# Layer 0 of a scan-and-memory kernel: m's norm by rows in eight blocks, and group statistics in steps a unit apart

## The chip, the cores and the metric

The kernel runs on one core of a Trainium2 chip. Its time is the device time of one execution in microseconds (us); three timed runs gave 5054.97, 5055.22 and 5063.75, median 5055.22. [...]SP issues nearly all DMAs. The engines are called PE (TensorE), DVE (VectorE), ACT (ScalarE), POOL (GpSimd) and SP in the profile.

## The reference, cut to what matters

Two layers act on x of shape (2, 512, 64, 64), that is 2 batches, 512 channels and 4096 positions.

```python
x = x + mamba(gn(x))          # layer 0: a selective scan over the 4096 positions
x = x + memory(gn(x), m)      # layer 1: soft lookup in m (1024 rows of 512)

def gn(v):                    # 32 groups of 16 channels
    g = v.reshape(B, 32, 16, H, W)
    return ((g - mean(g)) / sqrt(var(g) + 1e-5)).reshape(v.shape)   # mean, var over a group and all positions

def memory(x, m):
    xn, mn = l2norm(tokens(x)), l2norm(m)      # l2norm divides each row by its length
    score = xn @ mn.T
    new_m = 0.999 * m + 0.001 * mean of the tokens whose best row it is
    return softmax(score) @ new_m
```

Two small pieces of this are what the change touches: mn, the rows of m divided by their length, which layer 1 needs as a matrix with channels on the partitions; and the mean and the inverse root of the variance of the 32 groups, once for each batch and each layer. All else stays.

## The kernel before, in words

Layer 0 is cut into 32 chunks of 256 positions (16 for each batch). A chunk is cut into 32 units: 8 blocks of 128 inner channels times 4 groups of 4 states. The number of a unit within its chunk is what "unit 12" means below. For each unit the main loop (from line 939) does the same things: `decay` writes exp(delta A) into PSUM on ACT (tile dA), one unit ahead; `feed` makes the scan's input on POOL (tile bu), four units ahead, with four buffers; `scan` runs the recurrence on DVE; `weigh` multiplies by C on DVE (tile hc, two buffers), or on POOL for units 2, 8, 12, 16 and 26; `gather` adds hc up on PE by transposes into tile yT. So hc can be written again only when PE has gathered what stood there two before, and a late PE stops DVE.

Everything else is placed between the units by a table of (unit, priority, function), built from line 911 on. `AT` (line 179) gives the units: the projections u and z of the next chunk (tile pz), the convolution (cv), the small projection (px), the layer norm of the chunk after that, the softplus of delta in eight steps (`d_mm` to `d_first`, with a series in tile q on POOL), and the output projection of the chunk before (po). The class `Queue` (line 26) stamps every instruction of layer 0 so that each engine keeps exactly the order in which they are written; this is why they all show line 36 in the profile, and tile names are used to tell them apart. Each engine thus works down one fixed queue, and an instruction that waits holds up all behind it.

Nearly all of these extra products share two PSUM buffers (tag "mm" of pool `ps`, line 203): a third tile waits until one of the two has been read for the last time.

`unit_m` (line 650) runs in four chunks, 8 to 11, for 256 rows of m each. It loads the transposed m (`mT`, channels on partitions), squares it on ACT, sums the squares over the channels by four matmuls with a constant matrix (tile pn), has the root on DVE and ACT, refines it by one Newton step on POOL (tile rm, 128x256), multiplies m by it on POOL (128x1024), and stores it to the DRAM tensor mnd. Its places are units 2, 28, 28, 30, 31 and 32, so that the last one falls into the next chunk.

`group_stats` (line 152) runs four times: for layer 0 at the start (batch 0) and at unit 12 of chunk 0 (batch 1), both through `stats_end` (line 215), which also makes gsh, the shift; and for layer 1 in `end` (line 630), at unit 23 of chunk 16 for batch 0 and behind the last chunk for batch 1. It joins the statistics of each channel on DVE (tiles gs_mv and gs_w), averages over the 16 channels of a group by a matmul (gs_pm), forms the spread on DVE (gs_d), averages that by a second matmul (gs_pv), takes the root on ACT and refines it on DVE (`rsqrt`, line 143). All of it is issued in one go, so that DVE's queue holds the steps back to back.

`clear` writes zeros over the two tables of layer 1 at unit 12 of chunk 1; it shares a tile with m.

Of the kernel before, what the change touches and what calls it, by code (L numbers as in the profile page):

```python
# [8 lines left out]
F32 = mybir.dt.float32  # L9
# [3 lines left out]
AF = mybir.ActivationFunctionType  # L13
# [5 lines left out]
P = 128  # L19
EPS = 1e-5  # L20
# [29 lines left out]
def kernel(  # L50
# [15 lines left out]
    mT: bass.AP,  # L66
# [76 lines left out]
    def rsqrt(nc, dst, var, work):  # L143

        nc.scalar.activation(dst, var, AF.Ln, bias=epsc)
        nc.scalar.activation(dst, dst, AF.Exp, scale=-0.5)
        nc.vector.tensor_mul(work, dst, dst)
        nc.vector.scalar_tensor_tensor(work, var, EPS, work, ALU.add, ALU.mult)
        nc.vector.tensor_scalar(work, work, -0.5, 1.5, ALU.mult, ALU.add)
        nc.vector.tensor_mul(dst, dst, work)  # L150

    def group_stats(nc, st, mu, rs, pool, psum):

        mv = pool.tile([P, CB, 2], F32, tag="gs_mv", name="gs_mv")
        for cb in range(CB):
            nc.vector.bn_aggr(mv[:, cb, :], st[:, cb].rearrange("p n s -> p (n s)"))
        w = pool.tile([P, CB, 2], F32, tag="gs_w", name="gs_w")
        pm = psum.tile([P, 2, T], F32, tag="mm", name="gs_pm")
        nc.vector.tensor_copy(w[:, :, 0], mv[:, :, 0])
        nc.tensor.matmul(pm[:, 0, :CB], gmat, w[:, :, 0], start=True, stop=True)  # L160
        nc.vector.tensor_copy(mu, pm[:, 0, :CB])
        d = pool.tile([P, CB], F32, tag="gs_d", name="gs_d")
        nc.vector.tensor_sub(d, mv[:, :, 0], mu)
        nc.vector.tensor_mul(d, d, d)
        nc.vector.tensor_add(d, d, mv[:, :, 1])
        pv = psum.tile([P, 2, T], F32, tag="mm", name="gs_pv")
        nc.tensor.matmul(pv[:, 0, :CB], gmat, d, start=True, stop=True)
        d2 = pool.tile([P, CB], F32, tag="gs_d2", name="gs_d2")
        rsqrt(nc, rs, pv[:, 0, :CB], d2)
# [4 lines left out]
    with ExitStack() as l0:  # L174
# [14 lines left out]
            "wo": (5, 1, 8, 7), "m": (2, 28, 28, 30, 31, 32), "gs": 12, "zo1": (-4, -3, -1, 3),  # L189
# [25 lines left out]
        def stats_end(b):  # L215
            group_stats(nc, st0, gmu[0][b], grs[0][b], s1, ps)
            nc.vector.tensor_mul(gsh[b], gmu[0][b], grs[0][b])
            nc.vector.tensor_scalar_mul(gsh[b], gsh[b], -1.0)
# [83 lines left out]
        stats_end(0)  # L302
# [288 lines left out]
        def back_fns(i):  # L591
# [38 lines left out]
            def end():  # L630
                if c == NCH - 1:
                    group_stats(nc, sts[b], gmu[1][b], grs[1][b], s1, ps)
                state[i].clear()
# [3 lines left out]
        def back(i):  # L637
# [10 lines left out]
            return parts + [(AT["end"], end)]  # L648

        def unit_m(q):  # L650

            s = {}
            cols = slice(q * T, (q + 1) * T)

            def load_m():
                s["m"] = s1.tile([P, CB, T], F32, tag="m", name="m")
                nc.sync.dma_start(
                    s["m"], mT[:, cols].rearrange("(cb p) k -> p cb k", p=P)
                )

            def square(h):
                sq = s1.tile([P, 2, T], F32, tag="sq", name="sqm")
                nc.scalar.activation(sq, s["m"][:, 2 * h : 2 * h + 2], AF.Square)
                if h == 0:
                    s["pn"] = ps.tile([P, 2, T], F32, tag="mm", name="pn")
                for j in range(2):
                    cb = 2 * h + j
                    nc.tensor.matmul(
                        s["pn"][:, 0], meanc, sq[:, j], start=cb == 0, stop=cb == CB - 1
                    )  # L670
# [557 lines left out]
```

## Time and profile before

| what | value |
|---|---|
| timed runs, median | 5055.22 us (5054.97 to 5063.75) |
| profiled execution, own time | 5066.93 us |
| its span | 5065.2 us, mean granted PE clock 0.966 |
| busy shares PE, PE weight load, DVE, ACT, POOL | 89, 69, 80, 70, 75% |
| layer 0, main loop | 130.2 to 3977.4 us |
| layer 1 | from about 3985 us to the end |
| chunk 0, chunk 1 | 149.8 and 117.4 us |

A line of a group in the profile gives the source line, the engine and operation, the output and input tiles, shapes and number, then busy time, mean duration, and idle time of that engine just before, with what ended the idle time. A line of the timeline gives start, duration, engine, operation, and in brackets the idle time before it and what ended that. A line of the table by stretches gives the stretch, its length, the busy time of PE, PE weight load, DVE, ACT and POOL with the number of instructions, the mean granted PE clock (1.00 is full speed), the share of the DMA engines that was busy and GB/s.

### The profile page before, as it was taken

The page shows a single profiled execution, that of the slowest core. Times are in us where ns is not written, and L with a number is a line of the kernel's source. Part 1 is how long each engine was busy: PE and PEld are TensorE (multiplying, and loading weights), DVE is VectorE, ACT ScalarE, POOL GpSimd, SP SyncE. Part 2 cuts the span into 40 slices and gives each one's busy share as a digit, 9 for nine tenths or more (in the row PEclk, how much of TensorE's full clock was granted, in tenths as well). Part 3 has the DMA queues.
Part 4 walks back from the last instruction along what each step waited for, and adds up shares of the span by engine and source line. Part 5 has one row for each costly group of instructions (what it writes and reads, how often), then busy time and mean ns, then how long its engine had stood idle before and what let it go on. Part 6 is the DMA issues. An engine that isn't in the chain of part 4 may idle for free. (4 is left out here: it accounts for less than half of the span.)

```text
span 5065.2 us, 64865 instructions
## 1 busy us (share of the span) xinstructions
PE 4523.6 (89%) x22704; PEld 3500.2 (69%) x22704; DVE 4048.3 (80%) x3390; ACT 3533.2 (70%) x8845; POOL 3822.4 (75%) x2825
## 2 busy tenths in 40 slices
PE   6888888988888899989898888888986899998999
PEld 5677777777777777777777777777775555553444
DVE  3699999999988999999999999999998755553010
ACT  1688888888888888878888888888886555551000
POOL 3799999999999999989999999999999322220000
PEclk9899999999999999999999999999997899998999
DMA  5022221122222212121122221221112344334453
GB/s 198 19 100 77 80 80 63 63 72 73 74 71 69 65 64 65 63 63 63 63 72 84 75 73 63 67 70 64 64 61 98 117 158 149 131 134 142 144 163 119
DMA packets 174400, 447.73 MB, mean 88 GB/s; under 512 B 23256, under 2 KB 77656, under 8 KB 169848
## 3 DMA queue, kind: packets, MB, share of 16 engines
q1 hardware_dynamic: 160384, 408.50, 24.0%
q0 software_dynamic: 10240, 34.61, 2.2%
q8 instruction: 179, 2.93, 0.2%
q14 instruction: 149, 1.22, 0.1%
q10 hardware_dynamic: 3448, 0.47, 0.1%
HBM read 351.63 MB, written 91.88 MB: 88 GB/s over the span
## 5 line engine op out<-in xcount | busy, mean ns | idle before, releaser
L36 POOL TENSOR_TENSOR bu<-B,du 128x1020 f32<-128x1020 f32 (+1 forms) x1152 | 2453.2, 2146 | 127.8 <-DVE dA L36 102.1
L36 ACT ACTIVATE dA<-delta,A 128x256 f32<-128x256 f32 x4096 | 1957.9, 478 | 150.5 <-DVE hc L36 39.8
L36 DVE TENSOR_TENSOR_SCAN dA<-dA,bu 128x1024 f32<-128x1024 f32 x864 | 1977.9, 2289 | 35.9 <-ACT dA L36 16.7
L36 PE MATMUL yT<-ident,hc 128*128 128x128 f32 x8192 | 1063.5, 278 | 193.0 <-DVE hc L36 109.8
L36 DVE TENSOR_TENSOR hc<-dA,C 128x1024 f32<-128x1024 f32 x864 | 1058.5, 1225 | 164.5 <-PE yT L36 76.0
L36 PEld LDWEIGHTS yT<-ident,hc 128*128 128x128 f32 x8192 | 950.2, 143 | 281.2 <-DVE hc L36 137.2
L36 PE MATMUL pz<-x,win 128*128 128x256 f32 x4096 | 938.5, 382 | 42.6 <-ACT bu L36 23.8
L36 PEld LDWEIGHTS pz<-x,win 128*128 128x128 f32 x4096 | 763.2, 191 | 153.4 <-POOL bu L36 27.8
L36 PE MATMUL po<-z,wo 128*128 128x256 f32 x2048 | 523.5, 414 | 1.8 <-DMA wo<-in_out_wT_dram 1.1
L36 PE MATMUL cv<-xi,cd 128*128 128x256 f32 x2048 | 473.6, 384 | 29.2 <-POOL xi L36 22.9
L36 PEld LDWEIGHTS po<-z,wo 128*128 128x128 f32 x2048 | 424.2, 210 | 83.3 <-issue 15.3
L1163 PE MATMUL po<-exT,win 128*128 128x512 f32 x1024 | 444.4, 597 | 20.3 <-DVE win L1146 14.3
L36 PEld LDWEIGHTS cv<-xi,cd 128*128 128x128 f32 x2048 | 382.1, 191 | 91.5 <-POOL xi L36 28.9
L1096 PE MATMUL pc<-win,xf 128*128 128x512 f32 x960 | 432.3, 592 | 0.0
L36 DVE TENSOR_TENSOR_SCAN h<-dA,bu 128x1024 f32<-128x1024 f32 x160 | 364.9, 2280 | 21.8 <-ACT dA L36 19.9
L1163 PEld LDWEIGHTS po<-exT,win 128*128 128x128 f32 x1024 | 196.1, 192 | 268.0 <-issue 268.0
L36 POOL TENSOR_TENSOR hc<-h,C 128x1024 f32<-128x1024 f32 x160 | 379.4, 2372 | 0.5 <-PE yT L36 0.5
L1070 POOL DMA_INDIRECT tab<-rows,ix x64 | 62.8, 982 | 418.2 <-DVE den L1111 398.6
L36 ACT COPY carry<-dA 128x4 f32<-128x4 f32 x810 | 130.1, 161 | 348.9 <-DVE hc L36 343.2
L1180 DVE TENSOR_TENSOR xt<-xt,po 128x512 f32<-128x512 f32 x64 | 44.0, 687 | 389.0 <-PE po L1163 373.2
L1096 PEld LDWEIGHTS pc<-win,xf 128*128 128x128 f32 x960 | 173.0, 190 | 172.2 <-issue 172.2
L36 PE MATMUL py<-ident,ys 128*128 128x128 f32 x512 | 85.8, 292 | 188.7 <-DVE q L36 70.0
(161 smaller groups left out, 5070.2 us busy)
## 6 DMA issues: line engine op xcount, KB each, us to landing
B<-bcd SPq DMA_DIRECT2D x128, 512.0 KB, 4.3
C<-bcd SPq DMA_DIRECT2D x128, 512.0 KB, 4.3
wo<-in_out_wT_dram SPq DMA_DIRECT2D x128, 512.0 KB, 5.0
exd<-exT SPq DMA_DIRECT2D x16, 2048.0 KB, 6.3
exT<-exd SPq DMA_DIRECT2D x16, 2048.0 KB, 9.2
xl<-in_x_dram SPq DMA_DIRECT2D x32, 512.0 KB, 6.3
x<-in_x_dram SPq DMA_DIRECT2D x32, 512.0 KB, 5.3
xo<-in_x_dram SPq DMA_DIRECT2D x64, 256.0 KB, 5.7
```

The source lines that it names most:

```text
L36: ins = call(*args, **kwargs)
L1070: nc.gpsimd.indirect_dma_start(tab, at, rows, None)
L1096: nc.tensor.matmul(pc[:, cols], xf[:, cb, i * P : (i + 1) * P], mn[:, cb, cols], start=cb == 0, stop=cb == CB - 1,)
L1163: nc.tensor.matmul(pos[j, cb], mrow[:, kb, cb * P : (cb + 1) * P], ld[j][0][:, kb], start=kb == 0, stop=kb == KB - 1,)
L1180: nc.vector.tensor_add(xt[:, cb], xt[:, cb], pos.pop((j, cb)))
```

## The change

m's norm is done by rows. Eight blocks of 128 rows are handled in chunks 8 to 15, one in each. A block is loaded as it lies (rows on partitions, 256 KB), squared on ACT with the sum of each row as by-product, so that the root and its Newton step work on one number for each partition (128x1, POOL and ACT). ACT then scales the rows, PE turns the block by four 128x128 transposes into an "mm" PSUM tile (ptm), ACT copies it out and SP stores it to mnd. The places are units 3, 12, 13, 14, 22 and 23. The input mT is gone.

`group_stats` returns a list of four steps: means, variances, roots, newton. The second and the fourth use the engine that is passed in: POOL for batch 1 of layer 0 and batch 0 of layer 1, DVE for the two that have nothing beside them. The variance is first copied from PSUM to SBUF by ACT. In chunk 0 the steps stand at units 12, 12, 13, 14, and the shift at 15; in chunk 16 at units 23, 24, 25, 26. From the second step on (in chunk 0 from the first on) they carry priority -1, so they come ahead of all else at their unit. `clear` uses a smaller tile (528 instead of 1024 columns).

```diff
+    def group_stats(nc, engine, st, mu, rs, pool, psum):
+        s = {}
+        def means():
+            mv = s["mv"] = pool.tile([P, CB, 2], F32, tag="gs_mv", name="gs_mv")
+            for cb in range(CB):
+                nc.vector.bn_aggr(mv[:, cb, :], st[:, cb].rearrange("p n s -> p (n s)"))
+            w = pool.tile([P, CB, 2], F32, tag="gs_w", name="gs_w")
+            nc.vector.tensor_copy(w[:, :, 0], mv[:, :, 0])
+            s["pm"] = psum.tile([P, 2, T], F32, tag="mm", name="gs_pm")
+            nc.tensor.matmul(s["pm"][:, 0, :CB], gmat, w[:, :, 0], start=True, stop=True)
+        def variances():
+            mv = s["mv"]
+            nc.vector.tensor_copy(mu, s.pop("pm")[:, 0, :CB])
+            d = s["d"] = pool.tile([P, CB], F32, tag="gs_d", name="gs_d")
+            engine.tensor_sub(d, mv[:, :, 0], mu)
+            engine.tensor_mul(d, d, d)
+            engine.tensor_add(d, d, mv[:, :, 1])
+            s["pv"] = psum.tile([P, 2, T], F32, tag="mm", name="gs_pv")
+            nc.tensor.matmul(s["pv"][:, 0, :CB], gmat, d, start=True, stop=True)
+        def roots():
+            nc.scalar.copy(s["d"], s.pop("pv")[:, 0, :CB])
+            s["v"] = s["d"]
+            nc.scalar.activation(rs, s["v"], AF.Ln, bias=epsc)
+            nc.scalar.activation(rs, rs, AF.Exp, scale=-0.5)
+        def newton():
+            work = pool.tile([P, CB], F32, tag="gs_d2", name="gs_d2")
+            v = s.pop("v")
+            engine.tensor_mul(work, rs, rs)
+            engine.tensor_scalar(v, v, 1.0, EPS, ALU.mult, ALU.add)
+            engine.tensor_mul(work, v, work)
+            engine.tensor_scalar(work, work, -0.5, 1.5, ALU.mult, ALU.add)
+            engine.tensor_mul(rs, rs, work)
+        return [means, variances, roots, newton]
...
-            "wo": (5, 1, 8, 7), "m": (2, 28, 28, 30, 31, 32), "gs": 12, "zo1": (-4, -3, -1, 3),
+            "wo": (5, 1, 8, 7), "m": (3, 12, 13, 14, 22, 23), "gs": 12, "zo1": (-4, -3, -1, 3),
...
+        def unit_m(kb):
+            rows = slice(kb * P, (kb + 1) * P)
             def load_m():
+                s["m"] = s1.tile([P, C], F32, tag="m", name="m")
+                nc.sync.dma_start(s["m"], m[rows])
+            def square():
+                s["ss"] = s1.tile([P, 2], F32, tag="mss", name="mss")
+                junk = s1.tile([P, ROW], F32, tag="mj", name="mj")
+                nc.scalar.activation(junk[:, :C], s["m"], AF.Square, accum_out=s["ss"][:, 0:1])
             def root():
+                ss, r = s["ss"][:, 0:1], s["ss"][:, 1:2]
+                nc.gpsimd.tensor_scalar(ss, ss, 1e-24, None, ALU.max)
                 nc.scalar.activation(r, ss, AF.Ln)
                 nc.scalar.activation(r, r, AF.Exp, scale=-0.5)
             def newton():
+                ss, r = s["ss"][:, 0:1], s["ss"][:, 1:2]
                 nc.gpsimd.tensor_mul(ss, ss, r)
                 nc.gpsimd.tensor_mul(ss, ss, r)
                 nc.gpsimd.tensor_scalar(ss, ss, -0.5, 1.5, ALU.mult, ALU.add)
                 nc.gpsimd.tensor_mul(r, r, ss)
+            def turn():
+                nc.scalar.mul(s["m"], s["m"], s["ss"][:, 1:2])
+                pt = s["pt"] = ps.tile([P, 2, T], F32, tag="mm", name="ptm")
+                pt = pt.rearrange("p a t -> p (a t)")
+                for cb in range(CB):
+                    nc.tensor.transpose(
+                        pt[:, cb * P : (cb + 1) * P], s["m"][:, cb * P : (cb + 1) * P], ident
+                    )
+            def store():
+                mt = s.pop("m")
+                nc.scalar.copy(mt, s.pop("pt").rearrange("p a t -> p (a t)"))
+                nc.sync.dma_start(mnd[:, :, rows], mt.rearrange("p (c k) -> p c k", k=P))
...
-        M_AT = [len(chunks) // 4 + q for q in range(K // T)]
+        M_AT = [len(chunks) // 4 + kb for kb in range(KB)]
...
+                parts = back(i - 1)
+                table += [(at + n, 4, fn) for n, fn in parts[:-3]]
+                table += [(at + n, -1, fn) for n, fn in parts[-3:]]
...
-        table.append((AT["gs"], 5, lambda: stats_end(1)))
+        table += [(AT["gs"] + max(n - 1, 0), -1, fn) for n, fn in enumerate(stats_end(1))]
```

## The prediction

> **What bounds the kernel now.** I read the page's 40 slices first. From slice 3 to slice 30 (layer 0) VectorE, GpSimd and TensorE all stand at 8 to 9 tenths and ScalarE at 8; TensorE alone sets the pace only after 3990 us. Slices are too coarse for this change, so I cut layer 0 at the first scan of each chunk (its start is in VectorE's timeline) and asked for busy times chunk by chunk. Below are chunks 6 to 13 and 16; the columns are the stretch, its length, then PE, PEld, DVE, ACT, POOL busy, granted clock, DMA.
>
> ```profile
> 867.80:986.20 118.40, 106.53 (x610) 91.73 (x609) 112.39 (x76) 100.46 (x260) 113.14 (x83) 0.97 0.21 68
> 986.20:1102.60 116.40, 103.40 (x610) 89.52 (x609) 112.29 (x75) 100.49 (x260) 113.05 (x83) 1.00 0.21 69
> 1102.60:1222.10 119.50, 107.72 (x623) 93.07 (x622) 112.94 (x77) 102.02 (x264) 115.69 (x86) 0.99 0.22 72
> 1222.10:1348.70 126.60, 112.37 (x618) 96.42 (x617) 113.10 (x76) 102.18 (x264) 117.95 (x88) 0.93 0.22 72
> 1348.70:1474.40 125.70, 111.43 (x617) 95.49 (x616) 113.07 (x75) 102.16 (x264) 117.84 (x88) 0.95 0.22 72
> 1474.40:1601.20 126.80, 112.54 (x618) 96.57 (x617) 113.14 (x76) 102.27 (x264) 118.00 (x88) 0.93 0.21 72
> 1601.20:1724.20 123.00, 108.57 (x604) 93.14 (x603) 112.47 (x74) 100.62 (x260) 115.38 (x85) 0.94 0.22 69
> 1724.20:1840.90 116.70, 104.82 (x610) 90.57 (x609) 112.36 (x75) 100.50 (x260) 113.11 (x83) 0.99 0.21 69
> ...
> 2075.30:2201.20 125.90, 109.50 (x623) 94.81 (x622) 115.87 (x88) 99.96 (x253) 113.39 (x78) 0.95 0.20 64
> ```
>
> The length column is the point. A plain chunk takes 116 to 118.4 us; the 14 chunks from 2201.2 to 3846.6 average 1645.4 / 14 = 117.5. In a plain chunk VectorE (112.4) and GpSimd (113.1) both have about 4 us to spare, ScalarE 17. Chunks 8 to 12, which hold m's old norm, take 621.6, that is 34.1 more than 5 x 117.5. Chunk 16, with the group statistics of batch 0, takes 8.4 more.
>
> Why 34? GpSimd gained only 3 x 0.73 + 0.41 + 2.36 = 5.0 us a unit (the rows of rm and m), 20 in all. TensorE's timeline early in chunk 10 shows the rest; the columns are start, duration, instruction, idle before it.
>
> ```profile
> 1362.75 1.09 PE L36 MATMUL yT<-ident,hc 128*128 128x128 f32 x8
> 1367.21 1.09 PE L36 MATMUL yT<-ident,hc 128*128 128x128 f32 x8 [3.37 <-POOL hc L36]
> ...
> 1372.43 5.20 PE L36 MATMUL cv<-xi,cd 128*128 128x256 f32 x16
> ```
>
> GpSimd, 5 us late, gives hc late; TensorE idles 3.37 us; its granted clock then reads 0.71 and 0.50 in the next two stretches of 3.4 us, so 16 matmuls take 5.20 instead of 3.62, and VectorE, which needs yT done before it may write hc again, stalls at units 6 and 7. So a delay of GpSimd is multiplied by the clock.
>
> For the statistics, VectorE in chunk 16:
>
> ```profile
> 2160.27 1.92 DVE L36 BATCH_NORM_AGGREGATE gs_mv<-st 128x2 f32<-128x96 f32 x4
> 2162.22 0.17 DVE L36 COPY gs_w<-gs_mv 128x4 f32<-128x4 f32 x1
> 2166.03 0.16 DVE L36 COPY gmu<-gs_pm 128x4 f32<-128x4 f32 x1 [3.63 <-PE gs_pm L36]
> ...
> 2168.81 2.29 DVE L36 TENSOR_TENSOR_SCAN dA<-dA,bu 128x1024 f32<-128x1024 f32 x1
> ```
>
> From 2160.35 to 2168.81 no scan runs: 2.1 us of aggregates, 3.6 waiting for the matmul behind the u projection, and 2.8 for the two roundtrips after it.
>
> **The change, part by part.**
>
> *m, removed.* All of the 34.1 us: both 0.42 us tensor_scalars and 5.0 us of GpSimd a unit, and the clock loss they cause.
>
> *m, added, per block, eight blocks in chunks 8 to 15.* ScalarE: Square 0.63 plus its accumulator read 0.19 (the rows of junk, lines 1030), Ln 0.26 and Exp 0.21 (the grs rows, 128x4), the scaling 0.59 and the copy from PSUM 0.59 (the row of xT, 128x512): 2.5 us. TensorE: four transposes, 0.14 apart as in the yT rows (8 in 1.09): 0.6. GpSimd: five operations on 128x1. No row has that shape; the ends are the 128x2 memset (0.10) and the 128x32 tensor_tensor (0.25), each plus the 0.08 that dependent GpSimd operations leave between them, so 0.9 to 1.65; I take the 128x6 copy (0.19), the nearest size: 1.35. SP: one 256 KB load at unit 3 and one 256 KB store at unit 23, half of what they were and twice as many; the load waits for nothing new, the store waits for the copy at 23, and behind it on SP stands nothing due before unit 24. Zero; without that cover the landing is some 5 us and still nobody needs m before unit 12.
>
> ScalarE has 17 us a chunk free, so its 2.5 are not a bound by themselves. What counts is who waits at the two places.
>
> *Units 12 to 17.* Behind the five small operations on GpSimd stand two feeds and the softplus series q. In chunk 15 (no stall before it):
>
> ```profile
> 2017.68 1.28 POOL L36 TENSOR_TENSOR q<-q,e 128x512 f32<-128x512 f32 x1
> ...
> 2019.30 0.67 DVE L36 SCALAR_TENSOR_TENSOR q<-lg,q 128x512 f32<-128x512 f32 x1
> ```
>
> q ends at 2018.96, VectorE asks at 2019.30: 0.34 to spare. With 1.35 more VectorE waits 1.0, and the hc of unit 18 some 0.2 more. ScalarE's square and roots (1.3) push the dA of unit 17 from 0.9 early to about 0.5 late: inside the same wait. But in every second chunk VectorE has already lost 2.38 us at unit 14 to the halved clock, and there q is 2.8 early: cost 0. In chunks like 13 (0.7 lost) it is about 0.3. With half the chunks of the first kind: 0.5 x 0 + 0.25 x 0.3 + 0.25 x 1.2 = 0.4.
>
> *Units 22 to 25.* The transposes need one of the two "mm" PSUM buffers. At unit 22 one holds z's last projection until unit 26, the other u's first until xi is copied at unit 23. So TensorE's transposes, issued at 22, wait for that copy, with the yT gathers of units 22 and 23 behind them; and ScalarE's store copy at 23 waits for the transposes, with the decay of unit 25 behind it. ScalarE in chunk 13:
>
> ```profile
> 1813.93 0.59 ACT L36 COPY xi<-pz 128x512 f32<-128x512 f32 x1 [1.17 <-PE pz L36]
> ...
> 1814.61 2.01 ACT L36 ACTIVATE dA<-delta,A 128x256 f32<-128x256 f32 x4
> 1816.56 0.58 ACT L36 COPY ys<-yT 128x512 f32<-128x512 f32 x1
> ```
>
> The scaling (0.59) fits into the 1.17 idle. Then: xi ends 1814.52, transposes done 1815.3 (0.07 + 0.7), copied 1816.0, the two small copies 1816.2, dA done 1818.2 instead of 1816.62. VectorE's scan of unit 25 starts at 1816.90 in the trace; it would start at 1818.3: 1.4 us a chunk. GpSimd uses the same 1.4 to win back its own delay, so no hc is late at units 28 and 4 and the old clock loss has no cause left.
>
> Does the wait halve the clock? [...]TensorE's new gaps are 0.7 before the transposes and about 1.5 before py (1.55 in the trace now, clock 1.00 in the stretch). [...]a gap of 2.06 us at unit 12 of chunk 14 is followed by 0.67 and 0.50. By that row 0.7 and 1.5 close together might count; the price would be the 2.4 us of the unit 14 stall, 8 x 2.4 = 19 us. I take nothing, since 1.55 passes, and keep the 19 for the range.
>
> Sum for m: 8 x (0.4 + 1.4) = 14.4 against 34.1: **-19.7**.
>
> *Group statistics, chunk 16.* VectorE keeps the aggregates, w and the copy of mu, 2.3 with a short wait; three small operations go to GpSimd at unit 24, five at 26. There GpSimd runs some units behind, so gs_pv comes late, and it holds the PSUM buffer until the copy at unit 25: u's second projection, with the gathers of 24 and 25 behind it, starts about 3.6 us later than in a plain chunk while VectorE is only 2.3 later. If TensorE stays at full clock that just fits (0); if it halves, VectorE waits some 2.5 at unit 27. I take the middle: 2.3 + 1.3 = 3.6 instead of 8.4 plus 0.3 in chunk 17: **-5.1**.
>
> *Chunk 0.* Steps one and two stand at the same unit, so the wait for gs_pm stays (it ends 198.85); but the scan now starts behind mu at 199.05 instead of 201.69: **-2.6**. The roots fall into ScalarE's idle 3.4 us there.
>
> *Start.* For batch 0 VectorE does it all as before, but through an extra ScalarE copy (0.27) and one more VectorE operation (0.2), with ScalarE's first normalization waiting for gsh: **+0.45**. At the end the same 0.45 runs beside TensorE's score matmuls (5.4 us in a row): 0. The smaller memset in chunk 1 is GpSimd time that nobody waits for: 0.
>
> Total -26.95. The profiled execution took 5066.9 us, 1.7 around its span of 5065.2; it would become 5040. The median is 11.7 below that execution, so the same difference gives **5055.2 - 27.0 = 5028.2**.
>
> **Rivals.**
> *All hidden.* m costs nothing and the statistics only VectorE's 2.3: -34.1 - 6.4 - 2.6 + 0.4 = -42.7, 5012. For it: ScalarE's 17 us of slack. Against: the PSUM buffer above is a plain wait.
> *The clock falls at units 23 to 25 in each block*: +19 on my sum, 5047. For it: the 2.06 gap. Against: 1.55 passes.
> *One stall for another.* The eight blocks cost in sum what the four did and only the statistics gain: -7, 5048, or no gain at all; near no change.
> *Slower.* Twice as many blocks at the old price of a unit, 34.1 / 4 = 8.5: late gathers at units 22 to 25 halve the clock for two stretches, which makes u's second projection (3.7 us) and the gathers late, then GpSimd's hc of unit 26, then the next chunk's unit 4. 8 x 8.5 - 34.1 - 7.2 = +27, 5082. It decides from (34.1 + 7.2 + 10) / 8 = 6.4 us a block. Against it: GpSimd gets 1.35 us now, not 5.
>
> **How the numbers follow.** Chances: forecast 0.55 (its own range 5018 to 5040), all hidden 0.20, clock falls 0.12, one stall for another 0.07, slower 0.06. 0.2% is 10 us, about what this kernel's measurement can tell from no change: under 5045 is faster, over 5065 slower. A third of the clock case lies under 5045, so faster 0.80, same 0.14, slower 0.06. The range runs from the low side of all hidden (5006) to the clock case and the mild end of the next (5050), leaving out under 2 in 10.
>
> **What would show it.** Chunks 8 to 15 each 118.5 to 120 long, chunk 12 no longer special; no clock loss at unit 5; a VectorE wait for dA of about 1.4 at unit 25 and ScalarE waiting for ptm; chunk 16 near 121; in chunk 0 a scan right after the copy of mu. I am wrong if the m chunks show 0.5 clock at units 24 to 26, if the small GpSimd operations take over 0.4 us each, or if VectorE's wait at unit 25 is absent.

## The result: 0.27% faster, half of what was forecast

| | before | after |
|---|---|---|
| timed runs, median | 5056.61 us (5047.7 to 5069.64, 6 runs) | 5043.27 us (5038.15 to 5044.94, 6 runs) |
| profiled execution, own time | 5066.93 us | 5044.94 us |
| its span, mean granted PE clock | 5065.2 us, 0.966 | 5043.1 us, 0.966 |

The ratio of the times is 0.9973, with a 95% interval of 0.9960 to 0.9985: 13.7 us gained, and between 7.6 and 20 by the interval. The forecast was 27.0 us, 5028.2. The sign is right, the time lies in the range on record, and the size is wrong by a factor of two.

The two profiled executions, cut at the same scans as in the prediction, stand like this (us):

| part | before | after | difference | predicted |
|---|---|---|---|---|
| start, to the first scan | 130.2 | 126.2 | -4.0 | +0.45 |
| chunk 0 | 149.8 | 147.3 | -2.5 | -2.6 |
| chunks 1 to 7 | 822.6 | 825.1 | +2.5 | 0 |
| chunks 8 to 15, m | 972.7 | 953.4 | -19.3 | -19.7 |
| chunks 16 and 17, statistics | 243.7 | 241.4 | -2.3 | -5.1 |
| chunks 18 to 29 | 1409.3 | 1411.9 | +2.6 | 0 |
| chunks 30 and 31 | 249.1 | 250.3 | +1.2 | 0 |
| layer 1 | 1087.8 | 1087.5 | -0.3 | 0 |

So in this one pair the main term looks exact, and still the medians moved by half of the forecast. The match is less than it seems: the execution before in this pair is the one from which the 34.1 us were read, so it cannot test that number. The contradiction is what the experiments had to resolve. First the parts, as the profile after shows them.

**m.** The table by stretches of the kernel after, chunks 8, 12, 14 and 16 (stretch, its length, busy PE, PE weight load, DVE, ACT, POOL, granted clock, DMA share, GB/s):

```profile
1098.50:1217.90 119.40, 108.02 (x618) 92.82 (x618) 112.37 (x74) 102.73 (x266) 115.21 (x89) 0.97 0.22 72
...
1576.20:1695.70 119.50, 107.30 (x614) 92.03 (x613) 112.46 (x76) 102.38 (x266) 114.36 (x88) 0.97 0.22 71
...
1814.00:1934.70 120.70, 110.10 (x619) 94.24 (x618) 112.40 (x75) 102.69 (x266) 114.86 (x88) 0.96 0.21 71
...
2052.00:2175.10 123.10, 111.03 (x623) 95.67 (x622) 114.44 (x81) 100.11 (x255) 115.25 (x87) 0.94 0.21 65
```

The reader is to see two things. The chunks of 125 to 127 us are gone: GpSimd's 118 has become 114 to 115, and the clock's 0.93 has become 0.97. And each of the eight m chunks still costs about 119.2 on average where a plain one (a chunk that holds none of the changed work) costs 117.5: 953.4 - 8 x 117.5 = 13.4 us for the new m.

Over half of those 13.4, 7.7 us, is lost at units 23 and 24 of the eight chunks, by the distances between VectorE's scans. Most of the rest, 3.9 us, is the stall of unit 14 by a halved clock, which six of the eight m chunks have but only six of the twelve chunks 18 to 29 of the same execution. Units 22 to 24 of chunk 10 show the first part. ScalarE's timeline (start, duration, engine, instruction, and in brackets the idle time before it and what ended it):

```profile
1428.72 0.59 ACT L36 COPY xi<-pz 128x512 f32<-128x512 f32 x1 [0.56 <-PE pz L36]
1430.06 0.59 ACT L36 COPY m<-ptm 128x512 f32<-128x512 f32 x1 [0.75 <-PE ptm L36]
...
1430.74 2.01 ACT L36 ACTIVATE dA<-delta,A 128x256 f32<-128x256 f32 x4
```

TensorE's timeline there:

```profile
1429.36 0.66 PE L36 MATMUL ptm<-ident,m 128*128 128x128 f32 x4 [0.68 <-ACT xi L36]
1429.86 1.91 PE L36 MATMUL yT<-ident,hc 128*128 128x128 f32 x16
1433.32 0.65 PE L36 MATMUL py<-ident,ys 128*128 128x128 f32 x4 [1.55 <-ACT carry L36]
```

and VectorE's:

```profile
1426.77 1.22 DVE L36 TENSOR_TENSOR hc<-dA,C 128x1024 f32<-128x1024 f32 x1 [0.46 <-DVE dA L36]
...
1430.93 1.23 DVE L36 TENSOR_TENSOR hc<-dA,C 128x1024 f32<-128x1024 f32 x1 [0.73 <-PE yT L36]
...
1432.78 2.30 DVE L36 TENSOR_TENSOR_SCAN dA<-dA,bu 128x1024 f32<-128x1024 f32 x1
```

The chain is the predicted one: xi is copied until 1429.31, only then do the transposes have their PSUM buffer (1429.36), the gathers queue behind them (1429.86), and ScalarE waits 0.75 for the transposes before it copies and makes the next decay. VectorE pays 0.73 at unit 24, waiting for the gathers, and its next scan starts at 1432.78, just as the late decay ends (1430.74 + 2.01 = 1432.75).

**Statistics in chunk 16.** TensorE after:

```profile
2148.71 0.81 PE L36 MATMUL py<-ident,ys 128*128 128x128 f32 x4 [3.33 <-ACT dA L36]
2149.32 0.42 PE L36 MATMUL gs_pv<-gs_d,gmat 128*128 128x4 f32 x2
2150.35 6.42 PE L36 MATMUL pz<-x,win 128*128 128x256 f32 x16 [0.61 <-ACT gs_d L36]
```

VectorE after:

```profile
2144.33 0.16 DVE L36 COPY gmu<-gs_pm 128x4 f32<-128x4 f32 x1
...
2158.12 1.22 DVE L36 TENSOR_TENSOR hc<-dA,C 128x1024 f32<-128x1024 f32 x1 [1.04 <-PE yT L36]
...
2163.33 1.23 DVE L36 TENSOR_TENSOR hc<-dA,C 128x1024 f32<-128x1024 f32 x1 [1.78 <-PE yT L36]
```

The 3.63 us wait for gs_pm is gone; the copy of gmu has no wait at all. But TensorE now idles 3.33 and then 0.61 us, the clock halves (0.50 from 2149.0 to 2155.8 us), and u's second projection takes 6.42 us where a plain chunk needs some 3.7. VectorE pays for it two and three units on: 1.04 + 1.78 = 2.8 us. The 3.33 us are not a wait for gs_pv: py has PSUM buffers of its own (tag "py"), which it shares with the tile that VectorE's q reads. VectorE's q, late by the aggregates, ends at 2148.56, and py starts at 2148.71.

**Chunk 0.** VectorE after:

```profile
193.62 1.64 DVE L36 COPY gs_w<-gs_mv 128x4 f32<-128x4 f32 x1
196.09 0.16 DVE L36 COPY gmu<-gs_pm 128x4 f32<-128x4 f32 x1 [0.83 <-PE gs_pm L36]
196.17 2.28 DVE L36 TENSOR_TENSOR_SCAN h<-dA,bu 128x1024 f32<-128x1024 f32 x1
```

The scan starts right behind the copy of gmu.

### The profile page after: what moved, and what is told of

It is laid out like the page before. It is cut to its first block, busy times and chain, and to the rows that moved or that the text cites. A ratio compares the mean times of both kernels' runs of the same rounds, so it can differ in the third digit from the quotient of the medians.

```text
span 5043.1 us, 64927 instructions
## 1 busy us (share of the span) xinstructions
PE 4522.5 (90%) x22704; PEld 3496.9 (69%) x22704; DVE 4043.8 (80%) x3372; ACT 3540.9 (70%) x8881; POOL 3825.4 (76%) x2863
## 3 DMA queue, kind: packets, MB, share of 16 engines
q14 instruction: 148, 1.21, 0.1%
## 5 line engine op out<-in xcount | busy, mean ns | idle before, releaser
L36 DVE TENSOR_TENSOR_SCAN dA<-dA,bu 128x1024 f32<-128x1024 f32 x864 | 1977.9, 2289 | 29.8 <-ACT dA L36 10.4
L36 PE MATMUL po<-z,wo 128*128 128x256 f32 x2048 | 534.6, 420 | 0.8 <-DVE z L36 0.8
L1191 PE MATMUL po<-exT,win 128*128 128x512 f32 x1024 | 444.4, 597 | 20.1 <-DVE win L1174 14.7
L36 DVE TENSOR_TENSOR_SCAN h<-dA,bu 128x1024 f32<-128x1024 f32 x160 | 364.7, 2280 | 19.3 <-ACT dA L36 19.3
```

Of the source, the lines that this page charges most:

```text
L36: ins = call(*args, **kwargs)
L1191: nc.tensor.matmul(pos[j, cb], mrow[:, kb, cb * P : (cb + 1) * P], ld[j][0][:, kb], start=kb == 0, stop=kb == KB - 1,)
```

## The experiments

Two theories stood at the start. **Size theory:** both the old and the new m cost what their profiles show, and the missing 13 us are lost somewhere that the change doesn't touch. **Clock theory:** the old m's 34.1 us are one draw out of several; what the late hc costs depends on where TensorE's idle gap falls against the steps of 3.413 us in which the traces record the granted clock, so other executions pay less and there was less to gain.

Below, a plain chunk is taken as 117.5 us, and the lengths of the parts are cut at the same scans in every run.

### The kernel before, profiled again

No edit; two more profiled executions.

> The kernel before, unchanged, for a second profile. The forecast took 34.1 us for m (chunks 8 to 12 over 117.5 us a chunk), 8.4 for the statistics in chunk 16 and a first scan at 130.2 us from one execution that was 10 us above the median. Theory A (m is cheaper in other executions): chunks 8 to 12 come out at 598 to 612 us instead of 621.6, all else within 3 us. Theory B (the 10 us lie elsewhere): chunks 8 to 12 again 619 to 624, and the execution is shorter before its first scan or in the plain chunks, or it is as long as the first.

> A third profile of the kernel before, unchanged. As for the second: by theory A chunks 8 to 12 sum to 598 to 612 us, by theory B to 619 to 624 with the difference at the start (first scan 126 to 131 us) or in the plain chunks.

The table by stretches gives chunks 8 to 12 as one row. The second of the two:

```profile
1103.10:1713.90 610.80, 543.64 (x3073) 469.40 (x3072) 565.48 (x376) 508.61 (x1312) 586.28 (x431) 0.96 0.22 73
```

610.8 us, and 621.6 in the first; the profile of the prediction had 621.7 by the same cuts. One kernel's m thus costs 34 or 23 us over 5 x 117.5 = 587.5.

Two more were taken later, to ask whether there are just these two patterns:

> A fourth profile of the kernel before, unchanged. Chunks 8 to 12 have come out at 621.7 and 621.6 in two executions and at 610.8 in a third. [...]this one lies within 2 us of 621.6 or of 610.8; a value between them, or under 605, speaks against two fixed patterns.

> A fifth profile of the kernel before, unchanged: as for the fourth, chunks 8 to 12 within 2 us of 621.6 or of 610.8. The execution is the longer the higher that sum.

The first of them, the same row:

```profile
1097.10:1701.60 604.50, 535.75 (x3073) 464.00 (x3072) 565.02 (x375) 509.05 (x1312) 584.48 (x431) 0.98 0.23 73
```

The second took 621.8. So 604.5 is a third value, and two fixed patterns are out. The excess is 34.2, 34.1, 23.3, 17.0 and 34.3 us in five executions of the same kernel, mean 28.6. The chip is not the reason: the second and third execution ran on one chip, the fourth and fifth on another, and each pair differs. VectorE, ScalarE and GpSimd are as busy in all (565, 509, 584 to 586); what differs is TensorE's busy time and its clock, 0.95 to 0.98. In the 604.5 execution TensorE's timeline in chunk 10, at the place shown in the prediction, is

```profile
1357.33 1.09 PE L36 MATMUL yT<-ident,hc 128*128 128x128 f32 x8 [2.20 <-POOL hc L36]
```

and the two stretches of 3.4 us behind it:

```profile
1357.40:1360.80 3.40, 3.40 (x19) 2.84 (x20) 3.27 (x3) 3.30 (x10) 3.40 (x2) 0.84 0.01 2
1360.80:1364.20 3.40, 3.40 (x15) 3.02 (x14) 3.31 (x3) 2.58 (x8) 3.26 (x7) 0.66 0.00 0
```

The clock reads 0.84 and 0.66 where the profile of the prediction had 0.71 and 0.50. This execution took 5044.25 us in all, no longer than the changed kernel's 5044.94.

These stretches lie across the steps of the clock's record. In that record, in every trace, the clock is either 1.00 or 0.50, and it changes only at the edges of steps 3.413 us long, which run through the whole execution as one grid. The first edge lies 0.05, 1.53, 2.82, 1.21 and 2.03 us behind the first instruction in the five executions, so the grid stands elsewhere against the program each time. Here one step is halved behind the gap (1359.72 to 1363.13 us), in the profile of the prediction two (1368.80 to 1375.62). Counted over chunks 8 to 12:

| execution | chunks 8 to 12 | over 587.5 | of it units 4 to 10 | of it units 29 to 31 | halved steps |
|---|---|---|---|---|---|
| of the prediction | 621.7 | 34.2 | 20.8 | 10.4 | 19 |
| second | 621.6 | 34.1 | 20.7 | 10.5 | 19 |
| third | 610.8 | 23.3 | 10.6 | 11.1 | 13 |
| fourth | 604.5 | 17.0 | 10.3 | 10.8 | 8 |
| fifth | 621.8 | 34.3 | 20.8 | 10.6 | 19 |
| old m with the new statistics, below | 610.0 | 22.5 | 5.8 | 10.6 | 14 |

(The columns of units compare the distances between scans with their mean in chunks 18 to 29 of the first five.) The excess follows the number of halved steps (correlation 0.98, 1.64 us for each), and a halved step withholds half of 3.413, 1.71 us. So it is the part at units 4 to 10 that varies with the clock; what the two columns leave is mostly unit 14, a clock stall that plain chunks have as well. The 10.4 to 11.1 us at units 29 to 31 are in every execution and are another thing: VectorE waits there for m's matmuls and for late decays. In chunk 10 of the prediction's profile:

```profile
1465.57 0.43 DVE L36 TENSOR_SCALAR rm<-pn 128x256 f32<-128x256 f32 x1 [0.89 <-PE pn L36]
1466.40 2.30 DVE L36 TENSOR_TENSOR_SCAN dA<-dA,bu 128x1024 f32<-128x1024 f32 x1 [0.40 <-ACT dA L36]
...
1474.44 2.30 DVE L36 TENSOR_TENSOR_SCAN dA<-dA,bu 128x1024 f32<-128x1024 f32 x1 [0.88 <-ACT dA L36]
```

0.89 + 0.43 + 0.40 + 0.88 = 2.6 us in each of four chunks.

That the place of the grid matters shows in a gap that both executions have at unit 0 of chunk 10. TensorE in the profile of the prediction, then in the fourth execution:

```profile
1353.02 0.63 PE L36 MATMUL py<-ident,ys 128*128 128x128 f32 x4 [2.49 <-ACT dA L36]
```

```profile
1343.07 1.08 PE L36 MATMUL py<-ident,ys 128*128 128x128 f32 x4 [2.49 <-ACT dA L36]
```

and the clock, now cut at the edges of the steps, for the first:

```profile
1351.73:1355.14 3.41, 2.13 (x18) 2.13 (x19) 3.34 (x3) 2.68 (x8) 3.35 (x4) 1.00 0.00 0
1355.14:1358.56 3.41, 3.41 (x19) 2.98 (x18) 3.39 (x3) 2.03 (x6) 3.41 (x3) 1.00 0.32 107
```

and for the fourth:

```profile
1339.24:1342.65 3.41, 1.34 (x13) 1.10 (x11) 3.32 (x3) 3.31 (x11) 3.20 (x4) 1.00 0.37 130
1342.65:1346.07 3.41, 3.00 (x14) 3.03 (x15) 3.32 (x3) 1.81 (x4) 3.35 (x4) 0.50 0.00 0
```

The same 2.49 us of idle time are parted by an edge into 1.20 and 1.29 in the first, and the clock stays at 1.00. In the fourth 2.07 of them lie in one step, and the next step is halved.

### Does the delay of GpSimd cause it?

In the kernel before, the large scaling on GpSimd is moved away from the softplus work and the early hc, eight units later, and the load of m moves with it. All work stays.

```diff
-            ... "m": (2, 28, 28, 30, 31, 32), ...
+            ... "m": (14, 28, 28, 30, 31, 40), ...
```

> The kernel before with its old norm of m, but the load moved to unit 14 and the scaling on GpSimd moved from unit 32 to unit 40, so that the same 5.0 us of GpSimd a unit of m fall into two lots eight units apart. If the clock multiplies one long delay of GpSimd (theory: late hc, TensorE idle over 2 us, half clock), chunks 8 to 12 fall from 611 to 622 us to 597 to 603, with no clock loss between units 0 and 5. If it is the GpSimd and VectorE work itself that costs, they stay above 608.

The same row by stretches for this kernel:

```profile
1103.30:1705.20 601.90, 536.72 (x3073) 463.10 (x3073) 565.05 (x376) 508.25 (x1312) 586.06 (x431) 0.98 0.23 74
```

601.9 us for chunks 8 to 12 with GpSimd as busy as before (586), as the clock theory had it. TensorE's gap ahead of unit 4 in chunk 10:

```profile
1359.42 1.09 PE L36 MATMUL yT<-ident,hc 128*128 128x128 f32 x8 [1.15 <-POOL hc L36]
```

1.15 us instead of 3.37 or 2.20, and no clock is lost there: the four matmuls yT<-dD,u that follow take 0.71 us, where they took 1.22 in the profile of the prediction and 0.97 in the fourth execution. Units 4 to 10 cost 3.2 us over plain, less than in any row of the table above (5.8 to 20.8), while units 29 to 31 keep their 10.7. The expectation of no clock loss between units 0 and 5 did not hold in two chunks: chunks 11 and 12 have a halved step at unit 1, behind the gap at unit 0, and chunk 11 took 123.7 us. It is one execution, and 604.5 stands without the edit, so it supports the step from late hc to clock, not its size.

### The two parts alone

The kernel before with the new m and its old statistics, 22 executions:

```diff
-            ... "m": (2, 28, 28, 30, 31, 32), ...
+            ... "m": (3, 12, 13, 14, 22, 23), ...
...
-        M_AT = [len(chunks) // 4 + q for q in range(K // T)]
+        M_AT = [len(chunks) // 4 + kb for kb in range(KB)]
```

with the new `unit_m` and the smaller tile of `clear`; and the kernel after with the old `unit_m`, its places and its `clear` (the same lines the other way round), 14 executions.

> The kernel before with m's norm by rows alone; the group statistics in one go as before. By the forecast's sum -19.7 us in chunks 8 to 15 (each 118.5 to 120 long), a ratio near 0.996. If m's old norm cost less in most executions than in the one profiled (theory A), the timed ratio is nearer 0.998 to 0.9985 while the profile still shows 119 to 120 for each of chunks 8 to 15. Chunk 16 stays at 124 to 127 and chunk 0 at 148 to 151.

> The kernel after with the old norm of m put back; the group statistics in steps alone. By the forecast's sum -5.1 (chunks 16 and 17), -2.6 (chunk 0) and +0.45 at the start: -7, ratio 0.9985. By what the profile of after showed (chunk 16 at 123.1, TensorE at half clock behind gs_pv) only -2.3 and -2.5: -5, ratio 0.999. Chunks 8 to 12 cost what they cost before, 119 to 127 each.

| | median | ratio to before | 95% interval |
|---|---|---|---|
| m alone | 5050.13 us | 0.9979 | 0.9971 to 0.9987 |
| statistics alone | 5055.49 us | 0.9992 | 0.9982 to 1.0001 |
| both, the change | 5043.27 us | 0.9973 | 0.9960 to 0.9985 |

m brings 0.21%, 10.6 us (6.6 to 14.7); the statistics 0.08%, 4 us, with an interval that touches no change. Their sum, 0.29%, agrees with the 0.27% of both within these intervals, so the runs show no loss between them. In its profile m alone has 954.0 us in chunks 8 to 15, 14.0 over plain. If m gains 10.6 in the timed runs and costs 14.0 after, it cost about 25 before (an estimate; 21 to 29 by the interval): between the profiles' 17 and 34, and not 34.1. The statistics alone are also a sixth profile of the old m, the last row of the table above.

The 35 timed runs of the kernel before in that comparison spread from 5051.35 to 5081.49 us (standard deviation 7.1) and follow their mean granted clock (0.962 to 0.967, correlation -0.68); those of the statistics alone, which keep the old m, spread by 6.1 (-0.68); those of m alone by 3.3 and hardly follow it (-0.27). That fits an old m whose cost varies with the clock and a new one whose cost varies less.

### What is left of m: the turn one unit later

The waits at units 22 to 24 come from transposes issued before their buffer is free. Here turn and store stand a unit later, and the store comes ahead of that unit's other work.

```diff
-            ... "m": (3, 12, 13, 14, 22, 23), ...
+            ... "m": (3, 12, 13, 14, 23, 24), ...
...
-                table += [(at + n, 5, fn) for n, fn in unit_m(M_AT.index(i))]
+                table += [(at + n, 0 if n == AT["m"][-1] else 5, fn) for n, fn in unit_m(M_AT.index(i))]
```

> The kernel after with the transposes of m at unit 23, behind the copy of xi that frees their PSUM buffer, and the copy out and store at unit 24, ahead of u's second projection. If the 1.1 us that VectorE loses at units 23 and 24 of each chunk from 8 to 15 come from the PSUM buffer and the copy that waits for the transposes, those two units go back to 3.53 and 4.13 us and chunks 8 to 15 fall from 953 to 943 to 947. If they come from ScalarE's added time (0.72 and 0.59), they stay.

ScalarE in chunk 10:

```profile
1431.77 2.01 ACT L36 ACTIVATE dA<-delta,A 128x256 f32<-128x256 f32 x4
...
1434.19 0.58 ACT L36 COPY m<-ptm 128x512 f32<-128x512 f32 x1
```

The decay no longer stands behind the copy, and the copy waits for nothing. Chunks 8 to 15 take 948.0 instead of 953.4, a little over the 943 to 947 expected; timed 5036.25 us, 0.9954 (0.9938 to 0.9969), which overlaps the interval of the change, so the timed runs alone do not settle the gain. Unit 24 goes from 4.87 us to between 4.14 and 4.58, but unit 23 stays at 3.88 where a plain one takes 3.53. That 0.36 (the 0.46 gap of VectorE above) is in every version made from the changed kernel; with m alone seven of the eight chunks have 3.63 at unit 23 and 5.12 or 5.13 at unit 24, nearly the same loss in sum. A unit of 3.89 also occurs without the new m (unit 21 of chunk 7 in the kernel before), so it need not come from m, and it stays unexplained.

### Chunk 16: small operations on VectorE, closer together

Theory: py and u's projection are late only because gs_pv comes late from GpSimd and holds the buffer.

```diff
-                engine = nc.vector if i == last else nc.gpsimd
+                engine = nc.vector
...
-            return parts + [(AT["end"] + n, lambda n=n: step(n)) for n in range(4)]
+            return parts + [(AT["end"] + at, lambda n=n: step(n)) for n, at in enumerate((0, 1, 1, 3))]
```

> The kernel after with the small operations of chunk 16 on VectorE and the roots at unit 24 right behind the second matmul (newton stays at 26), so that GpSimd's queue is no part of it and the PSUM buffer is free a unit sooner. If GpSimd's place and the held buffer make TensorE idle and halve its clock, chunks 16 and 17 fall from 241.4 to 237.5 to 239.5 us in spite of 1.5 us more on VectorE. If the aggregates on VectorE are all that costs, they rise to 242 to 243.

TensorE in chunk 16:

```profile
2150.86 1.09 PE L36 MATMUL py<-ident,ys 128*128 128x128 f32 x4 [4.29 <-DVE q L36]
2152.42 6.05 PE L36 MATMUL pz<-x,win 128*128 128x256 f32 x16 [0.25 <-ACT gs_d L36]
```

Chunks 16 and 17 took 243.8 us, longer than the 241.4 of the changed kernel and than the 239.8 to 242.6 of the five other executions with its statistics, and the theory fell: TensorE idles even longer before py (4.29 us). VectorE's q ends at 2150.71 with the small operations ahead of it, py starts at 2150.86, as in the changed kernel 0.15 us behind q, and the projection again takes 6.05 us where a plain chunk needs some 3.7. So it is mainly VectorE's lateness that makes TensorE idle here, and neither GpSimd's place nor the buffer of gs_pv. VectorE's own list holds a surprise that belongs to the section on the hardware below. It is one execution, of 5045.95 us.

### The same gap in plain chunks: an output projection moved, then cut

If gaps of TensorE cost clock, plain chunks should pay as well. In the kernel after, at unit 12 of chunk 18, TensorE's timeline:

```profile
2338.89 1.09 PE L36 MATMUL yT<-ident,hc 128*128 128x128 f32 x8 [2.07 <-DVE hc L36]
...
2341.69 6.32 PE L36 MATMUL po<-z,wo 128*128 128x256 f32 x16
```

2.07 us idle, then an output projection of 6.32 us, with the clock at 0.50 from 2341.0 to 2344.4. First that projection (eight blocks, 16 matmuls) goes ahead of the gap:

```diff
-            "back": ((2, 6, 8, 11), (2, 12, 14, 18)), ...
+            "back": ((2, 6, 8, 11), (2, 11, 14, 18)), ...
```

> The kernel after with the third block of the output projection issued at unit 11 instead of 12, ahead of the gather that TensorE idles 2 us for. No work is added or taken. If that idle time is what halves the clock at unit 12 in nearly every chunk and stalls VectorE at unit 14 by 0.6 or 2.3 us, the clock stays at 1.00 there, unit 14 takes 3.53 in all chunks and a plain chunk 116.0 to 116.6 on: 25 to 40 us less, about 5010, and the m chunks no longer lock at 119.43. If the clock falls for another reason, or the projection waits itself, the time stays at 5040 to 5046.

TensorE's timeline in chunk 18 is then:

```profile
2336.10 3.62 PE L36 MATMUL po<-z,wo 128*128 128x256 f32 x16
...
2344.26 3.89 PE L36 MATMUL yT<-ident,hc 128*128 128x128 f32 x16 [1.98 <-DVE hc L36]
```

The projection takes 3.62 us and unit 14 is undisturbed, but the idle time is only moved: 1.98 us now ahead of unit 14's gathers, which run at half clock (3.89 for 16 transposes that take 1.91 at full), and VectorE waits at unit 17 instead. 5033.37 us, 0.9950 (0.9936 to 0.9963), far from the 5010 expected. Chunks 18 to 29 took 1409.6 us with 21 halved steps. In the eleven profiles in which these chunks have the unmoved projection they took 1407.2 to 1411.9 with 13 to 18 halved steps, so the profile shows no gain here; where the timed gain over the changed kernel lies is not shown.

Then the projection is cut in two, half ahead of the gap and half behind it:

```diff
-                    (k0, lambda cp=cp: load_x(cp)), (k, lambda cp=cp: mm(2 * cp)),
+                    (k0, lambda cp=cp: load_x(cp)),
+                    (k - cp, lambda cp=cp: mm(2 * cp, range(DB // 2))),
+                    (k, lambda cp=cp: mm(2 * cp, range(DB // 2, DB))),
```

> The kernel after with only half of the third output block issued at unit 11 and the other half left at 12. With the whole block at 11 TensorE's idle time of 2 us went from unit 12 to unit 14 and halved the clock there. If it is one gap of about 2 us that halves the clock, two gaps of about 1 us do not: no clock loss at units 12 to 14, unit 14 at 3.53 and unit 17 at 4.92, plain chunks 116.0 to 116.8 and the time at 5010 to 5022. If it is the sum of idle time within a stretch of several units, the loss stays and the time is 5033 to 5044.

TensorE's timeline in chunk 18 with the cut:

```profile
2337.54 1.09 PE L36 MATMUL yT<-ident,hc 128*128 128x128 f32 x8 [0.32 <-DVE hc L36]
...
2343.50 1.09 PE L36 MATMUL yT<-ident,hc 128*128 128x128 f32 x8 [1.44 <-DVE hc L36]
2345.42 1.09 PE L36 MATMUL yT<-ident,hc 128*128 128x128 f32 x8 [0.83 <-POOL hc L36]
```

The same work, and no less idle time in sum (0.32 + 1.44 + 0.83 = 2.6 us), but in three pieces, and the chunk keeps its clock, by its row in the table by stretches:

```profile
2292.10:2408.50 116.40, 103.47 (x609) 89.33 (x608) 112.41 (x75) 100.33 (x260) 112.97 (x83) 1.00 0.22 69
```

against, in the kernel after,

```profile
2293.40:2411.90 118.50, 106.34 (x609) 91.49 (x608) 112.41 (x76) 100.29 (x260) 113.28 (x83) 0.97 0.20 68
```

Timed 5027.83 us, 0.9936 (0.9921 to 0.9950), faster than the changed kernel; against the projection merely moved, the intervals overlap. The time lies between the two expectations. Chunks 18 to 29 took 1402.5 us with 7 halved steps, 4.7 to 9.4 less than the eleven profiles named above. Some of them still have a halved step at units 9 or 14, so the gap was not the only one.

### The two that helped, together

The later turn and the cut projection, both edits as above.

> The same half block at unit 11, and the transposes of m at unit 23 with the copy out at 24. On top of the half block some 5 us less in chunks 8 to 15, as in the version with the late transposes alone. By the first reading of the clock 5003 to 5017, by the second 5028 to 5038.

5025.1 us (5016.87 to 5031.43, 6 runs), 0.9932 (0.9920 to 0.9945), faster than the kernel before and than the changed one. In its profiled execution (5022.01 us) chunks 8 to 15 take 944.9 and the mean clock is 0.975. Against the cut projection alone, timed beside it, the intervals overlap: the 6.8 us that the later turn takes off chunks 8 to 15 in the profiles (951.7 to 944.9) are not settled by these timed runs. The result is over the 5003 to 5017 that adding up both gains gave and under the 5028 to 5038 of the second reading, so it bears neither out. Chunks 18 to 29 have 9 halved steps here (1404.4 us), a second execution below the 13 to 18 of the uncut projection.

## Why the prediction was right or wrong

**m, removed: the step that failed, by its size.** The step reads "All of the 34.1 us". The mechanism held for the larger part: take the delay of GpSimd from the early hc, and units 4 to 10 cost 3.2 us instead of 5.8 to 20.8. But 34.1 was the cost in one execution, and near the top of what was found: five profiled executions give 17.0 to 34.3, mean 28.6, and the timed runs of m alone imply about 25. The prediction's own rows had the sign of it. The clock was in them as 0.93 and 0.95, and the number of halved steps, 8 to 19, differs with nothing changed in the program. The reason given for the 34.1, GpSimd's delay times the clock, also left out the 10.4 us of VectorE's waits at units 29 to 31; they were inside the sum, so this cost the number nothing.

In the timed runs the terms account for most of the miss. The forecast of 27.0 was 13.3 over the measured 13.7: the old m cost about 9 less than taken (25 for 34.1), the statistics brought 3 less (4 for 7.3), and the new m cost what was taken within 1.

**The sum set on the median: the second part of the same error.** "so the same difference gives 5055.2 - 27.0" took a difference read in an execution that was 11.7 us over the median and subtracted it from the median. If an execution is long because its clock losses are, part of what is to be removed is already absent from the median. The fourth execution is such a case the other way round: 22.7 us shorter in all than the first, 17.2 of it in chunks 8 to 12. Against its own execution the sum did well: for the touched parts after the start, -27.4 predicted, -24.1 in the pair; the whole pair moved by 22.1. With the mean of five, 28.6, in place of 34.1, the same working gives 14.4 - 28.6 = -14.2 for m, inside what m alone measured (-6.6 to -14.7).

**m, added: 14.4 predicted, 13.4 measured, in part by luck.** The small operations on GpSimd took 0.19 each as taken, the copy from PSUM 0.59, the scaling 0.72 instead of 0.59; the groups of the kernel after (busy sum, mean ns, idle before) are

```profile
L36 POOL TENSOR_TENSOR mss<-mss 128x1 f32<-128x1 f32 x24 | 4.6, 192 | 1.3
L36 ACT ACTIVATE m<-m,mss 128x512 f32<-128x512 f32 x8 | 5.7, 717 | 0.0
```

ScalarE waited 0.75 in each block for ptm, as named. VectorE's loss is 1.1 (0.36 at unit 23, 0.74 at unit 24) where 1.4 was predicted at unit 25: the place was read one step too far down the chain, since the gathers behind the transposes stop VectorE before the late decay does. By the letter a sign of being wrong came true, for VectorE's wait for dA at unit 25 is absent (0.03 us). The other term, 0.4 a chunk for VectorE's wait for q behind unit 14, was right in size for another reason: that wait grew by 0.2 in two chunks only, and 3.9 us came from the clock stall of unit 14, which more of these chunks had than was taken. Chunks 8 to 12 were each 119.4 to 119.5, inside 118.5 to 120, but chunks 13 to 15 took 118.3, 120.7 and 117.3, outside it; chunk 12 is no longer special, unit 5 loses no clock. That 1.55 us of TensorE idle before py costs nothing, the choice against the rival of a falling clock, held.

**Statistics, chunk 16: 3.6 predicted, and the bad end came.** Both ends were stated, "0" and "some 2.5" for VectorE's wait, and the middle was taken. The projection did run at half clock (0.50, 6.42 us), and VectorE waited 2.8. Of TensorE's idle time, 0.61 us is the wait for the buffer of gs_pv that was named; the 3.33 before it are the wait for VectorE's q, 1.55 us of which a plain chunk has too, and the experiment without GpSimd's part did not bring the clock back. Chunk 16 took 123.1 where "near 121" was forecast, and the pair shows -2.3 for chunks 16 and 17. Here the profile of before was a cheap draw: the five profiles give 243.7, 246.9, 247.7, 243.6 and 247.5, mean 245.9, against which the kernel after gains 4.5 (its 241.4 is one draw too; with the old m it was 242.0). Timed, all the statistics together bring 4 us (-1 to 9), where -5.1 - 2.6 + 0.45 = -7.3 was forecast.

**Chunk 0: right**, -2.5 for -2.6, by the predicted place; the seven profiles with the new statistics give 145.8 to 147.3, the five of the kernel before 149.3 to 149.8.

**The start** was predicted at +0.45. It varies by 5 us between executions of the kernel before (125.2 to 130.2), so 0.45 can't be seen, and the -4.0 of the pair is no effect of the change.

**The rivals.** "All hidden" fell, since the wait for the PSUM buffer is there. "One stall for another" has a grain of truth in chunk 16 alone. "The clock falls at units 23 to 25" did not happen. What was not among the rivals is that the cost to be removed was not one number.

What stays open: how often each pattern of the old m occurs in timed runs (a timed run shows only its mean clock), how the place of the grid at the start leads to a pattern, and VectorE's 0.36 us at unit 23.

## What to carry to other kernels

When the cost that an edit removes is in part clock loss, profile the unchanged kernel several times before its cost is read: here one stage cost 17 to 34 us in five executions, and the first was a high one. Set a sum against the execution it was read from, and don't subtract a difference of a long execution from the median of others. And when TensorE has an idle gap that can't be removed, cut the work beside it so that the gap falls apart into pieces: in chunks 18 to 29 that left 7 and 9 halved steps in two profiles where the uncut work had 13 to 18, and moving the work past the gap left 21.

## What the runs showed of the hardware

**How short a gap loses the clock.** The length of a gap alone does not decide it. Gaps of 1.98, 2.07 and 2.20 us lost clock in the places shown (gathers of 3.89 instead of 1.91, a projection of 6.32 instead of 3.62, stretches at 0.84 and 0.66), and so did 2.49 us in one execution; in another the same 2.49 us lost none, and neither did 1.55, 1.44 and 1.15 in the places shown. TensorE's idle time within one step of the 3.413 us grid sorts the clear cases. Counted over chunks 1 to 30 of all fourteen traces, for the steps at full clock: with under 0.8 us idle none of 11,006 was followed by a halved step; with 0.8 to 2.02 us, 300 of 2,576; with more, all 209. In the profiles of before and after alone that is none of 1,559, 43 of 379 (the least idle time that was followed by one is 1.02 us) and all 29. The ends of matmuls are modelled in the profile, so these bounds are rough. What tells the 300 apart stays open: the 2.20 us, parted by an edge into 1.19 and 1.02, lost a step, and the 1.20 and 1.29 of the other execution did not.

**Five equal chunks.** Chunks 8 to 12 after take 119.42 to 119.43 us each, and 35 steps are 35 x 3.413 = 119.46. So each chunk starts a little earlier within its step (0.81, 0.76, 0.72, 0.68 and 0.65 us behind an edge), and each has the same two halved steps, which begin 47.0 to 47.1 us after its start and make unit 14 last 5.81 us. It is a slow drift and not a lock; in chunk 13 one of the two is gone, and unit 14 takes 4.12.

**Small VectorE operations that end with one of GpSimd's.** With the small operations of chunk 16 on VectorE, two of five took over 1 us:

```profile
2154.16 1.22 DVE L36 TENSOR_TENSOR gs_d<-grs 128x4 f32<-128x4 f32 x1
2155.31 0.15 DVE L36 TENSOR_SCALAR gs_d<-gs_d 128x4 f32<-128x4 f32 x1
2155.50 1.11 DVE L36 TENSOR_TENSOR gs_d<-gs_d,gs_d 128x4 f32<-128x4 f32 x1
...
2156.85 0.17 DVE L36 TENSOR_TENSOR grs<-grs,gs_d 128x4 f32<-128x4 f32 x1
```

GpSimd's timeline at the same place:

```profile
2153.00 2.36 POOL L36 TENSOR_TENSOR bu<-B,du 128x1020 f32<-128x1020 f32 x1 [1.72 <-DVE dA L36]
2155.33 1.26 POOL L36 TENSOR_TENSOR delta<-delta,q 128x512 f32<-128x512 f32 x1
```

The two long ones end at 2155.38 and 2156.61, within 0.02 us of the ends of GpSimd's two operations (2155.36 and 2156.59); the one between them took 0.15 (it started 0.02 us before GpSimd's second), and the last, with GpSimd idle, 0.17. The copy of gs_w in chunk 0 after (1.64 instead of 0.17) ends in the same way, at 195.26, 0.03 us after GpSimd's du (193.98 + 1.25 = 195.23). A busy GpSimd alone does not decide it: in chunk 16 after, the copy of gmu from gs_pm took 0.16 (2144.33 to 2144.49) in the middle of GpSimd's q (2143.79 to 2145.06). No run varied GpSimd's work alone, so why they end together is not shown. On VectorE these three operations of 128x4 thus took 1.11 to 1.64 us beside a busy GpSimd, where with GpSimd idle such an operation took 0.16 to 0.17; on GpSimd itself one took 0.19 to 0.20.
